# Segment sums of a graph layer: each 128-node tile gathered from three edge blocks by half products into one PSUM bank, instead of one window product per block

## The chip, the cores and the metric

The kernel runs on one core of a Trainium2 chip. The metric is the device time of one execution in microseconds, lower is better. Three runs of the kernel before took 2466.66, 2468.91 and 2469.73 us, so the median is 2468.91 us.

## What is computed

One layer of a graph network over 6250 nodes with 256 channels and 100,000 edges, sorted by their target node, followed by a mixture of experts whose gate is a second graph attention over 131,072 other edges. The part that the change touches is the segment sum in the first half:

```python
msg = relu(x[src] + edge_attr @ We + be)            # one row of 256 per edge
aggr = segment_sum(msg, dst, num_segments=6250)     # rows added up by target node
z = x + aggr
h = relu(relu(z @ W1 + b1) @ W2 + b2) + x           # then a layer norm
```

A linear attention and a wide MLP (the "mixer") run on the same nodes. Their sum is normalised and goes to the second half: a table of 20 numbers per node, gathered once per edge of the second graph, and four experts per node.

## The kernel before

**Stages.** The trace has three parts. Up to about 104 us the nodes are normalised and written to memory, as rows to be gathered (`xb_d`) and as the starting values of the sums (`z0_d`). From there to about 1277 us comes the *edge stage*, which this document is about. It does the edge messages, the sums, the attention, the mixer MLP, the node MLP (`graph_mlp`) and a bitonic sort of the second graph's edge keys, all interleaved. From 1278 us on the second half gathers 784 times from the table `tab_d`, which the edge stage completes as its last act.

**Blocks.** Edges are cut into tiles of 128 and blocks of eight tiles (`EG = 8`); there are 99 blocks (`NQ`). The edge list is shifted by half a block so that block `q` always falls into a fixed *window* of 128 nodes that starts at node 64·(q−1). There are 49 tiles of 128 nodes (`NT`). An odd block `q` covers exactly tile `q // 2`; an even block covers the second half of tile `q // 2 − 1` and the first half of tile `q // 2`. So a tile `k` takes rows from blocks 2k, 2k+1 and 2k+2.

**One block, step by step.** GpSimd (POOL) gathers the source rows, 128 at a time, by indirect DMA (L408, `gather_four`, four to a buffer `xg`, four buffers). TensorE multiplies edge attributes by `We` (L1241) into one of two PSUM buffers `msg`. VectorE adds the gathered rows (L1227, `m`), which frees the `xg` and the `msg` buffer. ScalarE applies the relu (L1229). TensorE then adds up the rows of each tile by slot, with the one-hot matrix `S` (L1259): eight products with 32 columns each fill the four 32-partition quarters of one bank. ScalarE copies that bank to `left` (L1263). `W` is a one-hot matrix of 128 by 128 which places the 128 slots in the window (L1215; for even blocks with the two halves of its columns exchanged, `iotah`). The *window product* `W.T @ left` (L1266) yields the 128 rows of the window in a bank `win`, and VectorE adds them to the sum tile `z` (L1188): one add of 128 rows for an odd block, two adds of 64 rows each for an even one. `graph_mlp` of a group of four node tiles (L1060 to L1176) starts when the last block of the group has been added.

**Order of work.** The engines run their instructions in the order in which the program emits them, and this order is written by a planner at build time (`Plan`, L65 to L130). Each thread of work yields steps with an engine, an assumed length, the slots it takes and drops (`bank`, `left`, `W`, `xg` ...), and names it needs and gives. The planner keeps a clock for each engine and always emits the step that can begin earliest; among steps of the same engine that can begin within 0.3 us (TensorE) or 0.15 us (others), the lowest `rank` goes first. `of_edges` makes the rank of edge steps 0 while the share of edge blocks begun is more than 6% behind the share of node work, and 6 otherwise; the mixer MLP has rank 6, `graph_mlp` rank 1, the sort −1 or 9. A change of a length, a rank or a slot count therefore reorders steps far from where it is made. Slots are counted by the planner, and the buffers behind them (`bufs=`) rotate on the chip, where semaphores hold the real waits. Four PSUM banks serve all products but the messages.

Of the kernel before, what the change touches and what calls it, by code (L numbers as in the profile page):

```python
# [8 lines left out]
F32 = mybir.dt.float32  # L9
# [8 lines left out]
P = 128  # L18
D = 256
# [15 lines left out]
GW = 4  # L35
EG = 8
# [10 lines left out]
PE, DVE, ACT, POOL, SP, MEM = range(6)  # L47
# [3 lines left out]
def mm(n, cols):  # L51
    return n * max(0.25, 0.00185 * cols)


def vec(cols, n=1):
    return n * (0.15 + 0.00105 * cols)


def act(cols, n=1):
    return n * (0.2 + 0.00084 * cols)  # L60


class Plan:
# [12 lines left out]
    def spawn(self, thread, at=0.0):  # L76
        step = next(thread, None)
        if step is not None:
            self.threads.append([thread, step, at, -1])
# [18 lines left out]
    def step(self):  # L98

        can = [(b, t) for t in self.threads for b in [self.begin(t)] if b is not None]  # L100
        if not can:
            assert not self.threads, [t[1] for t in self.threads]
            return False
        first, t = min(can, key=lambda c: c[0])
        near = first + (0.3 if t[1]["on"] == PE else 0.15)

        def rank(c):
            r = c[1][1].get("rank", 5)
            return r() if callable(r) else r

        b, t = min((c for c in can if c[1][1]["on"] == t[1]["on"] and c[0] <= near), key=lambda c: (rank(c), c[0]))
        thread, st = t[0], t[1]
        for k in st.get("take", ()):
            self.slots[k].remove(min(self.slots[k]))
        self.table = st.get("table") or self.table
        end = b + st["length"]
        self.free[st["on"]] = end
        t[2], t[3] = end + LAG[st["on"]], st["on"]
        at = len(self.threads)
        t[1] = next(thread, None)  # L120
        for k in st.get("give", ()):
            self.when[k] = t[2]
        for k in st.get("drop", ()):
            self.slots[k].append(t[2])
        for new in self.threads[at:]:
            new[2] = max(new[2], t[2])
        if t[1] is None:
            self.threads.remove(t)
        return True
# [7 lines left out]
def gps_layer_kernel(ctx: ExitStack, tc: tile.TileContext, a: dict, out: bass.AP):  # L137
    nc = tc.nc
    N = a["x"].shape[0]
    NQ = a["eaQ"].shape[0]  # L140
    NE = a["gat_dst"].shape[0]
    NT = (N + P - 1) // P
    NG = (NT + GW - 1) // GW
    NU = NQ * EG
    NUE = a["srcT"].shape[1]
    assert NUE % 2 == 0 and NU - EG < NUE <= NU
    CG = NE // P

    chunks = [(o, CW) for o in range(0, SURE - CW * P, CW * P)]
# [5 lines left out]
    def rows(t):  # L155
        return min(P, N - t * P)

    def group(g):
        t0 = g * GW
        nt = min(GW, NT - t0)  # L160
        return t0, nt, min(GW * P, N - t0 * P)
# [14 lines left out]
    def bank(name):  # L176
        return general[0].tile([P, 512], F32, tag="bank", name=name)
# [116 lines left out]
    WIN = P // 2  # L294
    EA, ZB = 3, 3
# [4 lines left out]
    ew = res.enter_context(tc.tile_pool(name="edge_w", bufs=3))  # L300
# [111 lines left out]
    XG = 4  # L412
    zs, eas, xgs = {}, {}, {}
# [78 lines left out]
    for g in range(NG + 3):  # L492
# [13 lines left out]
        if 0 <= g - 2 < NG:  # L506
            k = g - 2
# [3 lines left out]
            for o in range(KD):  # L511
                ps = bank("xmid")
                for c in range(KD):
                    nc.tensor.matmul(ps[:, :cols], wx[:, c, o * P:(o + 1) * P], yT[:, c, :cols],
                                     start=c == 0, stop=c == KD - 1)
                nc.scalar.activation(xm[:, o, :cols], ps[:, :cols], AF.Identity, bias=bx[:, o:o + 1])
        if 0 <= g - 3 < NG:
            k, cols = g - 3, group(g - 3)[2]
# [7 lines left out]
        if 0 <= g - 2 < NG:  # L526
            k, cols = g - 2, group(g - 2)[2]
# [34 lines left out]
        if 4 <= g < 8:  # L562
            s = slice(32 * (g - 4), 32 * (g - 4) + 32)
# [8 lines left out]
    for o in range(KD):  # L572
        nc.tensor.matmul(pr[:, o * P:(o + 1) * P], kmax[:, o:o + 1].to_broadcast([P, P]), ident,
                         start=True, stop=True)
# [89 lines left out]
    def sort():  # L664
# [72 lines left out]
        for w in sorted({w for _, w in chunks}, reverse=True):  # L737
            first = [o for o, w_ in chunks if w_ == w]
            o0 = first[0]
            for o in first:  # L740
                if o == first[-1] or o + w * P not in first:
# [11 lines left out]
    xms.update({(0, g): x_mids[g] for g in first_order[:2]})  # L753
    R4, NXH = 7, 4
    plan = Plan(dict(bank=4, msg=2, xm=0, x=NXH, x_=1, hm=NXH, hm_=1, r4=R4, hT=1, qT=2, xn=1, mv=6,
                     xg=XG - 0, ea=EA, S=2, W=2, m=2, left=2, z=ZB))
    plan.when.update({("xm", 0, g): 0.0 for g in first_order[:2]})
    spawn = plan.spawn
    NODES = NT * 14.9
# [418 lines left out]

    kinds, mss = {}, {}

    def add_sums(pw, k, p0, p1):

        if not 0 <= k < NT:
            return
        p1 = min(p1, rows(k))
        if p0 < p1:
            z = zs[k // GW]
            nc.vector.tensor_add(z[p0:p1, k % GW, :], z[p0:p1, k % GW, :], pw[p0:p1, :D])  # L1188

    def sum_loads():  # L1190
        for g in range(NG):
            yield step(SP, 0.4, take=["z"], give=[("z", g)], rank=3)
            load_sums(g)
# [13 lines left out]
    def block_kinds():  # L1207

        for q in range(NQ):
            yield step(DVE, vec(256) + vec(64), take=["S", "W"], give=[("kinds", q)], rank=2)  # L1210
            S = ew.tile([P, EG, SLOT], F32, tag="S", name="S", bufs=2)
            nc.vector.tensor_tensor(S, iotaf[:, :SLOT].unsqueeze(1).to_broadcast([P, EG, SLOT]),
                                    slot[:, q * EG:(q + 1) * EG].unsqueeze(2).to_broadcast([P, EG, SLOT]), OP.is_equal)
            W = ew.tile([P, P], F32, tag="W", name="W", bufs=2)
            nc.vector.tensor_scalar(W, iotaf if q % 2 else iotah, spot[:, q:q + 1], None, op0=OP.is_equal)  # L1215
            kinds[q] = S, W

    def halves(q):
        return [(s, [i for i in range(4 * s, 4 * s + 4) if tile_ok(q * EG + i)]) for s in range(2)
                if tile_ok(q * EG + 4 * s)]  # L1220
# [22 lines left out]

    def sums():

        for q in range(NQ):
            hs = halves(q)
            tiles = [i for _, got in hs for i in got]
            assert len(tiles) % 2 == 0
            p0, p1 = tiles[0] // 2 * SLOT, (tiles[-1] // 2 + 1) * SLOT  # L1250
            yield step(PE, 1.1, need=[("m", q, s) for s, _ in hs] + [("kinds", q)], take=["bank"],
                       rank=of_edges, drop=["m"] * len(hs) + ["S"])
            S, W = kinds.pop(q)
            ps = bank("ps")
            ms = {s: mss.pop((q, s)) for s, _ in hs}
            for b in range(2):
                for i in tiles[b::2]:
                    j = i // 2
                    nc.tensor.matmul(ps[j * SLOT:(j + 1) * SLOT, :D], S[:, i, :], ms[i // 4][:, i % 4, :],  # L1259
                                     start=b == 0, stop=b == 1)  # L1260
            yield step(ACT, act(256), take=["left"], drop=["bank"], rank=0)
            left = ew.tile([P, D], F32, tag="left", name="left", bufs=2)
            nc.scalar.activation(left[p0:p1], ps[p0:p1, :D], AF.Copy)  # L1263
            yield step(PE, mm(1, 256), take=["bank"], drop=["left", "W"], rank=of_edges)
            pw = bank("win")
            nc.tensor.matmul(pw[:, :D], W[p0:p1, :], left[p0:p1, :], start=True, stop=True)  # L1266
            yield step(DVE, vec(256, 1 if q % 2 else 2), drop=["bank"], rank=1, give=[("sums", q)],
                       need=[("z", min(k // GW, NG - 1)) for k in ([q // 2] if q % 2 else [max(q // 2 - 1, 0), q // 2])])
            if q % 2:
                add_sums(pw, q // 2, 0, P)  # L1270
            else:
                add_sums(pw, q // 2 - 1, P // 2, P)
                add_sums(pw, q // 2, 0, P // 2)

    for thread in (block_loads(), gathers(), messages(), sums(), block_kinds(), node_loads(), sum_loads(),
                   mid_loads(), weights(), head_weights(), mid_weights(), mixer_mlp(), sort(), clears()):
        spawn(thread)
# [499 lines left out]
    spawn = plan.spawn  # L1777
# [88 lines left out]
def program(arrays):  # L1866
    import concourse.bacc as bacc

    nc = bacc.Bacc("TRN2", target_bir_lowering=False, num_devices=1)
    aps = {k: nc.dram_tensor(f"in_{k}", v.shape, mybir.dt.from_np(v.dtype), kind="ExternalInput").ap()  # L1870
           for k, v in arrays.items()}
    out = nc.dram_tensor("out", arrays["x"].shape, F32, kind="ExternalOutput").ap()
    with tile.TileContext(nc) as tc:
        gps_layer_kernel(tc, aps, out)
    return nc
# [9 lines left out]
```

## Time and profile before

| | |
|---|---|
| median of three runs | 2468.91 us |
| the profiled execution, its own time | 2467.7 us |
| its span, first to last instruction | 2465.9 us |
| mean granted TensorE clock | 0.912 |
| edge gathers (POOL, L408) | 782, mean 1017 ns, busy 795.1 us |
| window products (PE, L1266) | 99, two records each, busy 66.3 us in 128-row form |
| sum adds (DVE, L1188) | 147: 97 of 64 rows, 48 of 128, one each of 106 and 42; median 414 ns |
| copies of a block's slots (ACT, L1263) | 99, median 383 ns |

How to read it: "busy" is the time an engine spends in instructions. PE is TensorE's matmul, PEld its weight load, DVE VectorE, ACT ScalarE, POOL GpSimd and SP the engine that issues most plain DMAs. A float32 matmul of this kernel leaves two records, so "x8" is four products. An idle time is followed by an arrow and the instruction whose end released the engine; "issue" means that nothing in the profile held it. The chain of waits is followed back from the last instruction, at each step to what released it.

### The profile page before, as it was taken

The numbers are of one execution on the slowest core, as the hardware profiler recorded it, in microseconds if no ns is written. First come the engines' busy times: TensorE is split into PE (matmuls) and PEld (weight loads), VectorE is DVE, ScalarE is ACT, GpSimd is POOL, SyncE is SP. The second block draws the span as 40 slices with busy tenths as digits, with TensorE's granted clock in tenths as the row PEclk, the third lists the DMA queues.
The fourth block names the chain that finished last, engine by engine and source line by source line (L and its number), as shares of the span: only waits on it lengthen the run. The fifth ranks groups of instructions, "written<-read, shape, count | busy, mean of one in ns | idle before, by whom it ended". The sixth has DMA issues, their size and how long they took to land.

```text
span 2465.9 us, 30623 instructions
## 1 busy us (share of the span) xinstructions
PE 1997.3 (81%) x10156; PEld 1297.9 (53%) x10156; DVE 1590.8 (65%) x4328; ACT 898.9 (36%) x1429; POOL 1703.3 (69%) x1701
## 2 busy tenths in 40 slices
PE   6897889998899898999969999978578898986000
PEld 3484555565565565566546776644245565655000
DVE  7588886674687786888736771119757456426566
ACT  5544645555555455665521002112222131212001
POOL 5417777777677777777327777777777777777771
PEclk9998999999999998999989999989789999998555
DMA  8865457767655545554341111212335445224522
GB/s 261 283 198 177 141 156 226 225 192 241 205 148 152 159 132 166 155 149 122 93 133 25 13 46 52 62 45 78 85 95 181 113 137 167 67 57 113 176 50 72
DMA packets 243957, 329.65 MB, mean 134 GB/s; under 512 B 49504, under 2 KB 187010, under 8 KB 242374
## 3 DMA queue, kind: packets, MB, share of 16 engines
q1 hardware_dynamic: 176678, 209.82, 26.1%
q0 software_dynamic: 65776, 116.46, 19.1%
q8 instruction: 84, 1.38, 0.2%
q10 hardware_dynamic: 1328, 1.26, 0.2%
q14 instruction: 91, 0.75, 0.1%
HBM read 227.34 MB, written 100.04 MB: 133 GB/s over the span
## 4 chain that ended last, share of the span: by engine, by line
POOL 35%; PE 25%; issue 14%; DVE 10%; DMA 9%; ACT 2%; SPq 0%; DVEq 0%; POOLq 0%; ACTq 0%
POOL G L1329 22%; POOL xg L408 9%; DMA xg<-xb_d,srcI 6%; PE hist L1491 5%; PE ffn L1040 3%; DVE m L1227 3%; PE msg L1241 3%; PE ffn L1056 3%; PE e L1629 2%; POOL st_d L1563 2%; POOL gm L1653 2%; PE e L1611 2%; PE g L1093 1%; PE ps L1259 1%; PE g L1082 1%
## 5 line engine op out<-in xcount | busy, mean ns | idle before, releaser
L408 POOL DMA_INDIRECT xg<-xb_d,srcI x782 | 795.1, 1017 | 314.3 <-issue 208.1
L1329 POOL DMA_INDIRECT G<-tab_d,srcs x784 | 768.5, 980 | 317.5 <-issue 238.6
L1589 ACT ACTIVATE hT<-e,w_eb 128x512 f32<-128x512 f32 (+1 forms) x208 | 136.3, 661 | 732.8 <-PE e L1629 712.0
L1629 PE MATMUL e<-lT,ew 128*128 128x512 f32 (+1 forms) x832 | 365.9, 587 | 17.6 <-DMA lT<-xlT_d 10.4
L1611 PE MATMUL e<-ew,hT 128*128 128x256 f32 (+1 forms) x1568 | 364.4, 389 | 4.0 <-DVE yo L1593 1.6
L1611 PEld LDWEIGHTS e<-ew,hT 128*128 128x128 f32 (+1 forms) x1568 | 302.5, 195 | 68.8 <-issue 21.1
L1227 DVE TENSOR_TENSOR m<-msg,xg 128x1024 f32<-128x1024 f32 x196 | 234.1, 1217 | 128.3 <-DMA xg<-xb_d,srcI 78.0
L1229 ACT ACTIVATE m<-m 128x1024 f32<-128x1024 f32 x196 | 205.7, 1053 | 187.9 <-DVE m L1227 184.4
L1241 PE MATMUL msg<-we,ea 64*128 64x256 f32 x1564 | 225.6, 415 | 48.7 <-DVE m L1227 43.6
L1629 PEld LDWEIGHTS e<-lT,ew 128*128 128x128 f32 x832 | 153.7, 195 | 178.8 <-issue 152.6
L1593 DVE TENSOR_TENSOR yo<-e,b 128x256 f32<-128x256 f32 (+1 forms) x196 | 79.0, 419 | 233.2 <-PE e L1611 233.1
L1241 PEld LDWEIGHTS msg<-we,ea 64*128 64x128 f32 x1564 | 143.5, 194 | 130.3 <-DVE m L1227 88.7
L1341 PE MATMUL cT<-ident,T 128*4 128x128 f32 (+1 forms) x42 | 13.4, 319 | 223.1 <-DVE T L1411 70.4
L1040 PE MATMUL ffn<-yT,w_mW1T 128*128 128x512 f32 (+1 forms) x416 | 191.3, 587 | 1.0 <-ACT hT L1030 0.5
L1056 PE MATMUL ffn<-w_mW2T,hT 128*128 128x256 f32 (+1 forms) x784 | 187.5, 387 | 0.0
L1056 PEld LDWEIGHTS ffn<-w_mW2T,hT 128*128 128x128 f32 (+1 forms) x784 | 146.0, 191 | 36.9 <-issue 15.2
L1501 DVE TENSOR_TENSOR oh<-iotar,hl 128x1024 bf16<-128x1024 bf16 (+1 forms) x256 | 123.1, 555 | 43.4 <-PE hist L1491 43.4
L1491 PE MATMUL hist<-oh 128*64 128x128 bf16 x1024 | 125.7, 418 | 9.5 <-DMA b<-in_eb 9.5
L1341 PEld LDWEIGHTS cT<-ident,T 128*4 128x4 f32 (+1 forms) x42 | 3.6, 86 | 232.1 <-issue 121.0
L1259 PE MATMUL ps<-m,S 128*32 128x256 f32 x1564 | 110.0, 397 | 15.4 <-ACT yT L1018 7.7
L1491 PEld LDWEIGHTS <-oh 128*64 128x64 bf16 x1024 | 101.6, 198 | 37.0 <-issue 12.6
L1040 PEld LDWEIGHTS ffn<-yT,w_mW1T 128*128 128x128 f32 x416 | 74.7, 195 | 73.6 <-issue 67.2
(382 smaller groups left out, 2909.9 us busy)
## 6 DMA issues: line engine op xcount, KB each, us to landing
ea<-in_eaQ SPq DMA_DIRECT2D x99, 256.0 KB
y_d<-yo SPq DMA_DIRECT2D x48, 512.0 KB
y<-y_d SPq DMA_DIRECT2D x48, 512.0 KB
sum_d<-zf SPq DMA_DIRECT2D x32, 512.0 KB
G<-tab_d,srcs POOLq DMA_INDIRECT x784
xg<-xb_d,srcI POOLq DMA_INDIRECT x782
xm<-xmT_d SPq DMA_DIRECT2D x23, 512.0 KB
sum_d<-G SPq DMA_DIRECT2D x11, 1024.0 KB
```

The source lines that it names most:

```text
L408: nc.gpsimd.indirect_dma_start(out=xg, out_offset=None, in_=xb_d[:, :], in_offset=bass.IndirectOffsetOnAxis(ap=srcI[:, u:u + 1], axis=0))
L1040: nc.tensor.matmul(ps[:, :cols], mw1[:, k, c * P:(c + 1) * P], yTs[g][:, k, :cols], start=k == 0, stop=k == KD - 1)
L1056: nc.tensor.matmul(ps[:r, :D], hT[0][:, c, i * P:i * P + r], mw2[:, c, :], start=c == 0, stop=c == MC - 1)
L1227: nc.vector.tensor_add(m[:, :n, :], ps[:, :n, :], xgs.pop(q * EG + 4 * s)[:, :n, :])
L1229: nc.scalar.activation(m[:, :n, :], m[:, :n, :], AF.Relu)
L1241: nc.tensor.matmul(ps[:, i % 4, :], lh, rh, start=True, stop=True)
L1259: nc.tensor.matmul(ps[j * SLOT:(j + 1) * SLOT, :D], S[:, i, :], ms[i // 4][:, i % 4, :], start=b == 0, stop=b == 1)
L1329: nc.gpsimd.indirect_dma_start(out=rows_of[o][:, c, :], out_offset=None, in_=tab_d[:, :], in_offset=bass.IndirectOffsetOnAxis(ap=srcs[:, o ...
L1491: nc.tensor.matmul(hist[0][b * KHI:(b + 1) * KHI, :P], hi[:, :, b * HG // 2 + i], lo[:, :, b * HG // 2 + i], start=c0 + i == 0, stop=c0 + ...
L1589: nc.scalar.activation(hT[:, c, :cols], ps[:, :cols], AF.Gelu, bias=b1[:, e * XC + c:e * XC + c + 1])
L1611: nc.tensor.matmul(ps[:r, :D], hT[:, c, i * P:i * P + r], w2s[e][:, c, :], start=c == 0, stop=c == XC - 1)
L1629: nc.tensor.matmul(ps[:, :cols], w1s[e][:, k, c * P:(c + 1) * P], lTs[g][:, k, :cols], start=k == 0, stop=k == KD - 1)
```

## The change

The window product and its adds are taken out of the loop over blocks. The loop now only keeps each block's `W` and `left`. Behind every even block from the second on, a new thread `by_node(k)` makes tile `k` whole: four products with 64 columns each (two column halves `h`, two terms `b`), each taking one half of a block's `W`, accumulate in one bank: rows 0 to 63 from blocks 2k and 2k+1, rows 64 to 127 from blocks 2k+1 and 2k+2. One add of all the tile's rows puts it in `z`. The TensorE step of `by_node` has rank 1 and an assumed length of 1.1 us; before, the window product had the rank of the edges and a length of 0.474 us per block. The buffers `left` grow from two to four and `W` from two to five. In the first and the last block, whose slots fill only 64 and 32 rows, `left` is first set to zero on VectorE, since the half products read all 128 rows. The name `("sums", q)` is given for even blocks only, which are the only ones that are asked for. No DMA is added, taken away or written differently.

```diff
-    plan = Plan(dict(bank=4, ..., S=2, W=2, m=2, left=2, z=ZB))
+    plan = Plan(dict(bank=4, ..., S=2, W=5, m=2, left=4, z=ZB))
...
-    def add_sums(pw, k, p0, p1):
-
-        if not 0 <= k < NT:
-            return
-        p1 = min(p1, rows(k))
-        if p0 < p1:
-            z = zs[k // GW]
-            nc.vector.tensor_add(z[p0:p1, k % GW, :], z[p0:p1, k % GW, :], pw[p0:p1, :D])
...
-            W = ew.tile([P, P], F32, tag="W", name="W", bufs=2)
+            W = ew.tile([P, P], F32, tag="W", name="W", bufs=5)
...
     def sums():
+        lefts = {}
+
+        def by_node(k):
+            yield step(PE, 1.1, take=["bank"], drop=["left", "W"] * 2, rank=1)
+            pw = bank("win")
+            for b in range(2):
+                for h in range(2):
+                    W, left = lefts[2 * k + b + h]
+                    s = slice(h * WIN, (h + 1) * WIN)
+                    nc.tensor.matmul(pw[s, :D], W[:, s], left, start=b == 0, stop=b == 1)
+            yield step(DVE, vec(256), drop=["bank"], rank=1, need=[("z", k // GW)], give=[("sums", 2 * k + 2)])
+            r = rows(k)
+            z = zs[k // GW][:r, k % GW, :]
+            nc.vector.tensor_add(z, z, pw[:r, :D])
...
-            yield step(ACT, act(256), take=["left"], drop=["bank"], rank=0)
-            left = ew.tile([P, D], F32, tag="left", name="left", bufs=2)
+            yield step(ACT, act(256), take=["left"], drop=["bank"], rank=0, give=[("sums", 0)] if q == 0 else [])
+            left = ew.tile([P, D], F32, tag="left", name="left", bufs=4)
+            if p1 - p0 < P:
+                nc.vector.memset(left, 0.0)
             nc.scalar.activation(left[p0:p1], ps[p0:p1, :D], AF.Copy)
-            yield step(PE, mm(1, 256), take=["bank"], drop=["left", "W"], rank=of_edges)
-            pw = bank("win")
-            nc.tensor.matmul(pw[:, :D], W[p0:p1, :], left[p0:p1, :], start=True, stop=True)
-            yield step(DVE, vec(256, 1 if q % 2 else 2), drop=["bank"], rank=1, give=[("sums", q)],
-                       need=[("z", min(k // GW, NG - 1)) for k in ([q // 2] if q % 2 else [max(q // 2 - 1, 0), q // 2])])
-            if q % 2:
-                add_sums(pw, q // 2, 0, P)
-            else:
-                add_sums(pw, q // 2 - 1, P // 2, P)
-                add_sums(pw, q // 2, 0, P // 2)
+            lefts[q] = W, left
+            if q and q % 2 == 0:
+                spawn(by_node(q // 2 - 1))
```

More of the change, by code (lines that the diff above doesn't have):

```diff
@@ L145, in gps_layer_kernel @@
     NUE = a["srcT"].shape[1]
-    assert NUE % 2 == 0 and NU - EG < NUE <= NU
+    assert NUE % 2 == 0 and NU - EG < NUE <= NU and NQ == 2 * NT + 1
     CG = NE // P
@@ L755, in gps_layer_kernel @@
     plan = Plan(dict(bank=4, msg=2, xm=0, x=NXH, x_=1, hm=NXH, hm_=1, r4=R4, hT=1, qT=2, xn=1, mv=6,
-                     xg=XG - 0, ea=EA, S=2, W=2, m=2, left=2, z=ZB))
+                     xg=XG - 0, ea=EA, S=2, W=5, m=2, left=4, z=ZB))
     plan.when.update({("xm", 0, g): 0.0 for g in first_order[:2]})
```

## The prediction

> **What bounds the kernel now.** I read the busy time by stage first, since the change touches only the edge stage (104 to 1277 us).
>
> ```profile
> core 0: us, PE busy (x) PEld busy (x) DVE busy (x) ACT busy (x) POOL busy (x), PEclk, DMA share, GB/s
> 155.00:300.00 145.00, 123.51 (x812) 84.26 (x811) 125.58 (x249) 77.76 (x124) 93.82 (x90) 0.94 0.55 163
> 450.00:600.00 150.00, 137.66 (x848) 85.14 (x844) 90.59 (x178) 83.75 (x127) 111.44 (x115) 0.97 0.75 227
> 750.00:900.00 150.00, 135.35 (x814) 86.59 (x815) 118.66 (x216) 80.17 (x121) 115.56 (x114) 0.94 0.50 146
> 900.00:1050.00 150.00, 137.02 (x822) 85.84 (x821) 121.33 (x230) 86.08 (x129) 115.84 (x113) 0.95 0.51 153
> 1211.00:1270.00 59.00, 57.28 (x248) 39.22 (x246) 27.45 (x81) 24.12 (x47) 0.00 (x0) 1.00 0.15 45
> ```
>
> POOL looks 77% busy, but 114 gathers in 150 us are one every 1.32 us, and the timeline of POOL shows 0.30 us of its own issue ahead of each. So 114 gathers of 1.014 us and 114 issues of 0.30 us make 149.8 of 150 us: from 750 to 1050 us POOL never waits. PE is 91% busy, DVE 80%. Who held POOL after 190 us:
>
> ```profile
> POOL xg L408 <- issue: 200.2, 657, 0.3
> POOL xg L408 <- DVE m L1227: 26.2, 21, 6.4
> POOL xg L408 <- DMA xg<-xb_d,srcI: 8.8, 29, 0.3
> ```
>
> Waits of 0.3 us are the issue time under another name. Real stops are only those above 0.5 us: 4.87 us ending at 373, 4.64 at 449, 4.12 at 535, 6.44 at 622 and 1.20 at 1091, together 21.3 us. Two earlier stops of 20.9 and 23.6 us end at 156 and 185 us; there the plan does the attention's first part ahead of the messages, and the sums have hardly begun (first add at 180 us). So the gather stream sets the pace until its last gather at 1200 us, and no help for DVE can bring the edges forward by more than 21 us. Behind it the last row of the table is a tail of TensorE work, 57.28 busy of 59 us, mostly mixer MLP left over by the plan's order. The second half starts when `tab_d` is complete and is again a stream of gathers (158 in each 200 us), unchanged, so what the edge stage gains or loses goes one to one into the time.
>
> **DVE's part: 98 adds fewer.**
>
> ```profile
> L1188 DVE TENSOR_TENSOR z<-z,win x147: 387/414/426, 180.2 to 1220.1; 64x256 f32<-64x256 f32 x97, 128x256 f32<-128x256 f32 x48, 106x256 f32<-106x256 f32 x1, 42x256 f32<-42x256 f32 x1
>   PE win L1266: 36.9, 25
> ```
>
> An add of 64 rows costs as much as one of 128 (418 and 412 ns in the groups by shape). Now 49 remain: 98 × 0.414 = 40.6 us of DVE are gone, 4% of the stage. The question is what of it lay on the path. I summed the pieces of the chain of waits from 104 to 1283 us, in short windows so that none is left out: POOL L408 212.6 us, the gathers' DMA 149.2, issue 136.4, PE L1040 75.5, DVE L1227 70.5; for what the change touches, PE L1266 17.4, DVE L1188 8.9, ACT L1263 0.7. Even the 8.9 is too much, as this piece of the chain shows:
>
> ```profile
> 1148.78 0.34 DVE z L1188
> 1149.13 0.06 issue
> 1149.18 4.18 DMA xg<-xb_d,srcI
> ```
>
> The chain goes from a gather to an add that has nothing to give it: a 0.3 us issue gap put down to whatever ended then. The list of POOL's waits has 8 such waits on L1188 (2.4 us in all); 8 × 0.41 = 3.3 us come off, leaving 5.6. Two thirds of the adds go (98 of 147): **−3.7 us**.
>
> Would fewer adds also make the gathers themselves shorter? They are stretched: after 190 us their time above 0.95 us adds up to 52.5 us. Rows of POOL and DVE side by side:
>
> ```profile
> 254.41 2.10 POOL L408 DMA_INDIRECT xg<-xb_d,srcI  x1 [0.30 <-issue]
> 254.41 0.68 DVE L677 TENSOR_TENSOR key<-key 128x512 f32<-128x512 f32 x1
> 199.51 0.95 POOL L408 DMA_INDIRECT xg<-xb_d,srcI  x1 [0.30 <-DMA xg<-xb_d,srcI]
> 198.31 2.34 DVE L1227 TENSOR_TENSOR m<-msg,xg 128x1024 f32<-128x1024 f32 x2
> ```
>
> Beside the sort's min and max, with both inputs in SBUF, a gather takes 2.10 us; beside the `m` add, one input in PSUM, 0.95. The Trainium skill (SBUF — State Buffer, "Who interferes with whom") says the same of instructions with at most one SBUF input, that they do not contend with GpSimd; it also infers that a two-input `tensor_tensor` spares descriptor generation, which these rows speak against. The removed add reads `z` from SBUF and `win` from PSUM, so it is of the sparing kind. If all of DVE's work stretched gathers alike, 52.5 × 40.6 / 805 (DVE busy, 155 to 1211 us) = 2.6 us would be gained; by row and rule it is 0. I take 0.
>
> **PE's part: 99 whole products become 196 half products.** From the start of a window product to the start of the next PE instruction, where PE did not idle, is 0.55 us (87 cases in the timeline): 99 × 0.55 = 54.5 us. No row shows a float32 product with 64 columns. From above: if the halves don't overlap, four at 0.43 us (a 256-column product at full clock: 32 of L1056 in 13.83 us) and 0.14 us around them are 1.86 us a tile. From below: two column halves run side by side, as the slot sums L1259 do with four quarters: eight products, 8 × 0.43 / 4 = 0.86 us of streaming, take 1.00 us from start to start (91 cases). A tile is then 4 × 0.43 / 2 = 0.86, and 0.14 for entering and leaving the narrower form: 1.00. L1259 has the same column tiling, alternating targets and bank, so I take 1.00: 49 × 1.00 = 49.0, PE −5.5 us. Of PE L1266 17.4 of 54.5 us (32%) lay on the chain: **−1.8 us**.
>
> A rule speaks against this: TensorEngine Tiling (Array Packing), "Key Properties", says that changing the tiling mode drains TensorE, and L1266 stood in the same 128x128 mode as most of its neighbours. It gives no price; TensorE: Matmul & The Clock Gate, "Single matmul latency", puts an isolated product at (398 + N) cycles against N, an estimate of 0.17 us a drain. Two drains a tile make 0.86 + 0.33 = 1.19 us, 58.3 us in all, +3.8 on PE, +1.2 on the chain: the total would be −2.5, no measurable change. The row has two such switches within its 0.14, so I keep the row.
>
> **The rest, at nothing.** Two memsets of 256 columns: between 0.06 us (128x8) and 0.46 us (128x480), under 1 us in all, off the gathers' path; if the last one came late it would hold one ACT copy of the last node tile, behind which 50 us of PE tail still run. 49 PSUM banks fewer are taken of four; PE's idle before L1259 (the next taker) is 15.4 us in all, so at most that, part of the same stalls; I take 0. The longer life of `left` and `W` is covered by four and five buffers: tile k holds three blocks, one more `left` and two `W` are free. The bank waits for ACT's newest copy: PE and PEld stood 8.5 us in 17 of 99 waits on it. By rank 1 the products now come right behind the copy. Bounds: none left (−8.5 × 0.32 = −2.7 on the chain), or 0.5 us at each of 49 tiles (24.5, +16 × 0.32 = +5). Behind them in PE's queue stand messages, behind those the `m` adds that free `xg`. I take 0, as there are half as many such waits. No DMA, SP or POOL instruction is moved by itself.
>
> **Sum.** −3.7 − 1.8 = −5.5 on the profiled execution's own 2467.7 us (span 2465.9 and 1.8 around it): 2462.2. The median of the runs is 1.2 us above that execution, so 2463.4.
>
> **Rivals.** Of this kernel no change under about 0.2% (4.9 us) can be told from none.
>
> *The gather stream hides it.* For: 149.8 of 150 us in mid-stage, and DVE itself waits for gathered rows (78.0 us in 34 waits of L1227). The 40 us turn into longer waits of that kind. 2468, from −4.9 to +4.9 of the median.
>
> *Slower: new stops of POOL.* The plan is dealt anew with shorter DVE and other ranks. The four stops of 4.1 to 6.4 us each come where two `m` adds stand in DVE's queue behind adds that wait for PE (L1104 behind L1093, 32.7 us in 7 waits). The new add waits for four products that wait for ACT, and stands at rank 1; L1188 already waited 36.9 us in 25 waits. Where it stands ahead of an `m`, POOL stops once its four buffers are full. Each stop costs about 5 us, so from two new ones on the sign turns; three give −5.5 + 15: 2478. Against: half as many adds, and most of mid-stage had no stop in spite of 147.
>
> *The halves don't overlap.* 49 × 1.86 = 91.1, +36.6 on PE, × 0.32 = +11.7, less 3.7: 2477. Against: L1259.
>
> *The old stops vanish too.* −5.5 − 20: 2443. Against: L1188 hardly takes part in them (one add of 0.42 us ahead of the first stop).
>
> **How the numbers follow.** Likeliest, 0.39: 2463.4, about 2453 to 2464. Hidden 0.28; new stops 0.22; no overlap 0.06; old stops gone 0.05. Faster 0.39 + 0.05 = 0.44, same 0.28, slower 0.28. The range runs from just inside the vanished stops, 2445, to four new stops, −5.5 + 20: 2484.
>
> **What would show it.** L1188's successor with 49 adds near 0.414 us and DVE some 40 us less busy; the half products at 1.00 us a tile from start to start; gathers unchanged near 1.02 us mean; POOL's stops after 190 us near 21 us, last gather near 1195 to 1200; the PE tail behind it near 60 us. I am wrong if stops come or go by more than 5 us, if the tail's length changes with the new order, or if a tile costs 1.5 us or more on PE.

## The result, and the profile after

The changed kernel takes 2489.01 us (median of four runs, 2485.28 to 2490.55) against 2468.25 us for the kernel before, run beside it (four runs): ratio 1.0089, 95% interval 1.0069 to 1.0109. It is 21 us slower, where 2463.4 was predicted and 2484 was the top of the range.

The profiled execution took 2490.55 us, its span is 2488.7. The busy time by stage, in the columns shown before, with two rows more: 950 to 1180 us, and the tail from the last edge gather to the second half. The changed kernel first:

```profile
core 0: us, PE busy (x) PEld busy (x) DVE busy (x) ACT busy (x) POOL busy (x), PEclk, DMA share, GB/s
155.00:300.00 145.00, 124.92 (x818) 87.58 (x818) 120.53 (x235) 74.37 (x122) 91.80 (x88) 0.92 0.52 159
450.00:600.00 150.00, 140.60 (x900) 84.29 (x901) 85.52 (x162) 84.85 (x130) 114.39 (x117) 0.97 0.77 230
750.00:900.00 150.00, 132.91 (x853) 83.38 (x853) 117.98 (x208) 80.86 (x121) 115.91 (x112) 0.96 0.49 145
900.00:1050.00 150.00, 132.07 (x864) 80.04 (x865) 116.00 (x219) 83.19 (x127) 115.03 (x115) 0.98 0.53 158
950.00:1180.00 230.00, 207.25 (x1326) 125.02 (x1325) 178.56 (x324) 133.59 (x201) 176.06 (x178) 0.98 0.49 146
1191.00:1301.00 110.00, 92.73 (x415) 61.30 (x413) 47.68 (x134) 46.39 (x85) 1.19 (x3) 0.96 0.16 47
```

The two added rows in the kernel before:

```profile
950.00:1180.00 230.00, 221.88 (x1366) 143.96 (x1366) 194.86 (x370) 138.95 (x211) 177.33 (x170) 1.00 0.48 143
1200.00:1278.00 78.00, 71.22 (x322) 46.22 (x320) 40.74 (x111) 34.20 (x67) 1.10 (x1) 0.97 0.18 50
```

The POOL column is nearly as before: gathers still set the pace. The PE column is what differs. From 950 to 1180 us TensorE is busy for 14.6 us less, and the tail behind the gathers holds 21.5 us more of its work. The POOL timeline shows the joint itself, first after, then before:

```profile
1191.38 0.95 POOL L408 DMA_INDIRECT xg<-xb_d,srcI  x1 [0.30 <-issue]
1300.83 0.94 POOL L1331 DMA_INDIRECT G<-tab_d,srcs  x1 [108.51 <-DVE iotar L1474]
```

```profile
1200.27 1.10 POOL L408 DMA_INDIRECT xg<-xb_d,srcI  x1 [0.30 <-issue]
1278.48 0.95 POOL L1329 DMA_INDIRECT G<-tab_d,srcs  x1 [77.12 <-DVE iotar L1472]
```

The last edge gather comes 8.9 us *earlier*, and the second half starts 22.4 us *later*. The tail has grown from 78.2 to 109.4 us. The second half itself takes 1187.9 us against 1187.4, so the joint holds the whole loss.

What the change meant to do, it did. The groups of VectorE, after, with the sums and with the message adds:

```profile
L1251 DVE TENSOR_TENSOR z<-z,win 128x256 f32<-128x256 f32 (+1 forms) x49 | 20.2, 413 | 21.5 <-DMA z<-z_d 11.5 <-PE win L1247 9.9
L1218 DVE TENSOR_TENSOR m<-msg,xg 128x1024 f32<-128x1024 f32 x196 | 236.8, 1219 | 177.7 <-DMA xg<-xb_d,srcI 125.8 <-PE ps L1266 42.5 <-PE win L1247 3.3
```

The 49 adds take 413 ns each, and VectorE is busy 1554.3 us instead of 1590.8. The relieved engine waits longer for gathered rows (125.8 us for 78.0). A tile of half products takes 1.01 us from its start to the start of the next TensorE instruction (median of the 39 cases without idle time).

One note on the runs below: e1 to e4 ran beside a kernel before at 2469.55 us (the *first setting*), while from e5 on the kernel before took 3651 to 3687 us with a mean granted clock of 0.77 to 0.78 (the *second setting*), so every ratio is to the kernel before that ran beside it on the same chip. The chip numbers on record are 15, 3, 10, 0 and 2 in the second setting and 0 for e1 to e4, so the record does not tell whether the chip or its condition makes the difference. In the second setting TensorE idles for up to 20 us at a time with no releaser in the trace (last section), and POOL is stopped for over 320 us in all after 190 us (19.8 before, in the first setting), so gathers do not set the pace there.

### The profile page after: what moved, and what is told of

It reads as the page before. It is cut to its first block, busy times and chain, and to the rows that moved or that the text cites. A ratio compares the mean times of both kernels' runs of the same rounds, so it can differ in the third digit from the quotient of the medians.

```text
span 2488.7 us, 30841 instructions
## 1 busy us (share of the span) xinstructions
PE 2005.8 (81%) x10350; PEld 1286.3 (52%) x10350; DVE 1554.3 (62%) x4232; ACT 905.2 (36%) x1434; POOL 1696.1 (68%) x1701
## 5 line engine op out<-in xcount | busy, mean ns | idle before, releaser
L408 POOL DMA_INDIRECT xg<-xb_d,srcI x782 | 788.0, 1008 | 312.0 <-issue 210.6
L1218 DVE TENSOR_TENSOR m<-msg,xg 128x1024 f32<-128x1024 f32 x196 | 236.8, 1219 | 177.7 <-DMA xg<-xb_d,srcI 125.8
L1056 PE MATMUL ffn<-w_mW2T,hT 128*128 128x256 f32 (+1 forms) x784 | 188.2, 387 | 0.7 <-ACT hT L1030 0.7
L1056 PEld LDWEIGHTS ffn<-w_mW2T,hT 128*128 128x128 f32 (+1 forms) x784 | 143.1, 189 | 42.4 <-issue 23.1
```

The lines of the kernel that those rows point to most:

```text
L408: nc.gpsimd.indirect_dma_start(out=xg, out_offset=None, in_=xb_d[:, :], in_offset=bass.IndirectOffsetOnAxis(ap=srcI[:, u:u + 1], axis=0))
L1056: nc.tensor.matmul(ps[:r, :D], hT[0][:, c, i * P:i * P + r], mw2[:, c, :], start=c == 0, stop=c == MC - 1)
L1218: nc.vector.tensor_add(m[:, :n, :], ps[:, :n, :], xgs.pop(q * EG + 4 * s)[:, :n, :])
```

## The experiments

**Which theory.** A: the re-dealt order costs the time. The half products' step has rank 1, where the window product had the rank of the edges (0 or 6). Edges run ahead of node work, and node work is left for the time behind the last gather. B, the rival: the new work itself costs the time (four products that wait for the newest copy, an add that waits for all four).

A can be put in a number without a run. In the emitted order of TensorE's instructions I counted the columns of all node products (mixer, attention, node MLP, with their transposes) behind the last message product, at 0.43 us for 256 columns, as in the 13.83 us for 32 of L1056. That is 59 us before and 85 us after. This number is called the *backlog* below. The two orders agree in this count up to about message tile 640 of 782, and part from there (162 against 171 us left at 640, 103 against 120 at 720).

### e1: the change's work in the order of before

```diff
...
+            whole = q % 2 == 0 and k >= 0
+            if whole:
+                pw = bank("win")
+                for b in range(2):
+                    for h in range(2):
+                        W_, left_ = lefts[2 * k + b + h]
+                        s = slice(h * WIN, (h + 1) * WIN)
+                        nc.tensor.matmul(pw[s, :D], W_[:, s], left_, start=b == 0, stop=b == 1)
...
```

The steps, lengths, ranks and slots of before; every even block emits the 4 half products and the one add, an odd block emits nothing. The cut parts are the change's buffers, its two memsets and the one add.

> The changed work (196 half products, 49 adds, two memsets) emitted at the planner's steps of the kernel before, so that every other instruction stands in the old order: 59 us of node products stand behind the last message product on TensorE, as before (85 in the changed kernel). Theory A (the new order costs the time, the new work itself saves some): 2459 to 2466 us, gathers end near 1191 to 1197 us, tail behind them near 78 us. Rival B (the half products, the memsets or the longer chain from three copies to one add cost the time): 2480 to 2492 us, as the changed kernel.

Measured: 2457.85 us (2445.87 to 2461.71), ratio 0.9951 (0.9934 to 0.9968). The POOL timeline at the joint:

```profile
1185.11 0.95 POOL L408 DMA_INDIRECT xg<-xb_d,srcI  x1 [0.30 <-issue]
1259.66 0.94 POOL L1337 DMA_INDIRECT G<-tab_d,srcs  x1 [73.61 <-DVE iotar L1480]
```

The tail is 74.6 us, as with the order before (78.2), and the last gather is 15 us earlier. B falls: the same work, in the old order, makes the kernel 12 us *faster*. (The execution with the trace, 2445.87 us, is the fastest of six, 12 us under their median; so the rows of e1 show more gain than its runs have in the middle.)

### e2: the removed adds put back

```diff
             nc.vector.tensor_add(z, z, pw[:r, :D])
+            n = min(r, WIN)
+            for _ in range(2):
+                nc.vector.tensor_add(pw[:n, D:], z[:n], pw[:n, :D])
```

The 98 added adds write into the unused half of the bank, and nothing reads them.

> The changed kernel in its own order, with two more adds of 64 rows by 256 per node tile on VectorE (98 in all), whose results go to an unused half of the PSUM bank and are not read; so VectorE has its old load in the new order. Theory A: the 40 us of adds are worth 0 to 9 us also here, so 2489 to 2498 us. Rival (VectorE's relief is what set the edges ahead and so made the tail longer on the chip): the time falls towards 2468.

Measured: 2501.44 us (2495.42 to 2503.9), ratio 1.0131 (1.0116 to 1.0147). That is 0.42% over the changed kernel by the two ratios, some 10 us, a little more than either theory said; the execution with the trace (2495.42 us, the fastest of four) is only 4.9 us over that of the changed kernel. The tail stays (110.4 us). So the adds are worth about as much in the new order as in the old, and the tail does not depend on them.

### e3: another assumed gather length

```diff
-            yield step(POOL, 5.0, take=["xg"], give=[("xg", u)])
+            yield step(POOL, 5.27, take=["xg"], give=[("xg", u)])
```

No work changes. Only the planner's clock of POOL runs slower, nearer to four gathers and four issues as measured (4 × (1.017 + 0.30) = 5.27 us). The backlog falls from 85 to 52 us.

> The changed kernel with one number of the planner changed: four gathers are assumed to take 5.27 us (4 x 1.317 as the trace of before has them) instead of 5.0. The work is the same; 52 us of node products stand behind the last message product instead of 85. Theory A: the tail gets shorter by about 20 to 33 us and the gathers end no more than 10 us later: 2456 to 2475 us. Rival B: 2485 to 2492.

Measured: 2440.91 us (2435.73 to 2448.03), ratio 0.989 (0.9873 to 0.9907), below the expected interval and faster than both kernels. The tail is 65.2 us, the last gather at 1181.3, and the stops of POOL after 190 us fall from 16.2 to 8.9 us. The order alone is worth 48 us against the changed kernel.

### e4: the kernel before, with rank 1 alone

```diff
-            yield step(PE, mm(1, 256), take=["bank"], drop=["left", "W"], rank=of_edges)
+            yield step(PE, mm(1, 256), take=["bank"], drop=["left", "W"], rank=1)
```

> The kernel before with one word changed: the window product's step has rank 1 as in the change, not the rank of the edges. The work is the kernel before's; 70 us of node products stand behind the last message product instead of 59. Theory A: slower by about 6 to 14 us, 2474 to 2482. Rival B: no change, 2466 to 2471.

Measured: 2492.48 us (2491.49 to 2493.35), ratio 1.0092 (1.0079 to 1.0105). Nothing of the change's work is in this kernel, and the loss is as large as that of the change. By stage (950 to 1180 us, and the tail):

```profile
950.00:1180.00 230.00, 212.23 (x1313) 134.93 (x1312) 187.82 (x349) 136.09 (x209) 174.29 (x171) 0.98 0.51 151
1206.00:1301.00 95.00, 81.35 (x349) 51.90 (x348) 43.16 (x122) 45.45 (x83) 0.51 (x1) 0.91 0.16 49
```

TensorE shows the pattern of the changed kernel: 9.7 us less busy than before from 950 to 1180, and 10.1 us more in the tail, with a tail of 95.8 us. It was slower than expected, because the tail's idle time grew too (13.7 us against 6.8), which the backlog does not count, and because the last gather came 5.3 us later, where the changed kernel has it 8.9 us earlier.

The runs of the first setting side by side, each from its execution with the trace. Stops are POOL's waits above 0.5 us after 190 us, less 0.3 us of issue each; gathers are L408's busy time:

| | backlog | stops | gathers | last gather | tail | second half starts | ratio |
|---|---|---|---|---|---|---|---|
| before | 59 | 19.8 | 795.1 | 1200.3 | 78.2 | 1278.5 | 1 |
| after | 85 | 16.2 | 788.0 | 1191.4 | 109.4 | 1300.8 | 1.0089 |
| e1 | 59 | 19.9 | 780.6 | 1185.1 | 74.6 | 1259.7 | 0.9951 |
| e2 | 85 | 15.9 | 795.1 | 1193.7 | 110.4 | 1304.1 | 1.0131 |
| e3 | 52 | 8.9 | 787.6 | 1181.3 | 65.2 | 1246.5 | 0.9890 |
| e4 | 70 | 22.2 | 795.0 | 1205.6 | 95.8 | 1301.3 | 1.0092 |

The last gather follows stops plus gathers: e1 has 14.5 us less of gathers and ends 15.2 us earlier; e3 has 18.4 us less of both and ends 19.0 earlier. The tail follows the backlog, with 13 to 26 us on top.

### The second setting: e5 to e18

Here the question was how far the backlog decides by itself. Times that were expected for the first setting could not be tried. (The expectation of e10 gives 395 us of stops for e6 and 308 to 323 for e5 and e7; counted as in the table above they are 476, and 355 and 387.)

**e5, e9, e15: 5.27 in the kernel before** (backlog 30; the edit of e3).

> The kernel before with one number changed: the planner takes 5.27 us instead of 5.0 for a gather of four; no work is changed. In the emitted order 30 us of TensorE node work stand behind the last message product, against 59 before. Theory A (the node work left behind the last gather is what decides): the last gather stays near 1195 to 1203, the tail to the second half falls from 78 to 45 to 55 us, the time is 2430 to 2452. Rival B (the gain with 5.27 came from something that only the new sums have, shorter gathers or half products): 2462 to 2475, no change.

> The kernel before with 5.27 us for a gather of four in the planner, again, on another chip: the first run stood on a chip on which the kernel before takes 3679 us and POOL is stopped 300 us in all by late TensorE and DVE. Node work behind the last message product: 30 us, against 59 before. Theory A (the node work left behind the last gather decides): tail 45 to 55 us, time 2430 to 2452. Rival B (the gain with 5.27 needs the new sums): 2462 to 2475.

> The kernel before with 5.27 us for a gather of four in the planner. Where the kernel before takes 3650 to 3680 us: 0.986 to 0.990 of it, as in two runs. Where it takes 2469 us: theory A (30 us of node work behind the last message product instead of 59) tail 45 to 55 us, 2430 to 2452; rival B (the gain with 5.27 needs the new sums) 2462 to 2475.

Measured: 3633.75, 3628.09 and 3638.79 us; ratios 0.9896 (0.9851 to 0.9941), 0.9863 (0.9836 to 0.9891) and 0.987 (0.9848 to 0.9893). The tails are 55.2, 56.6 and 55.0 us. Rival B of these runs, that the gain needs the new sums, falls at least in this setting.

**e6, e10, e12, e16: the changed kernel with the rank of the edges** (backlog 8).

```diff
-            yield step(PE, 1.1, take=["bank"], drop=["left", "W"] * 2, rank=1)
+            yield step(PE, 1.1, take=["bank"], drop=["left", "W"] * 2, rank=of_edges)
```

> The changed kernel with one word changed: the half products' step has the rank of the edges instead of 1; no work is changed. 8 us of TensorE node work stand behind the last message product. Theory A: with the rank of the edges the loss goes, and the tail is the shortest of all, 25 to 40 us. How far the last gather moves back is the question: if TensorE takes the node work in its idle time, it stays below 1215 and the time is 2405 to 2440; rival B (edges now come too late, POOL is stopped by TensorE, and the last gather moves back by what the tail loses): last gather 1230 to 1255, stops above 30 us, time 2445 to 2475.

> The changed kernel with the half products at the rank of the edges, on a chip where gathers set the pace. 8 us of node work stand behind the last message product. Theory A: tail 25 to 40 us, last gather below 1215, time 2405 to 2440. Rival B (edges come too late, POOL is stopped, the last gather moves back by what the tail loses): last gather 1230 to 1255, stops after 190 us above 30 us, time 2445 to 2475. On the slow chip POOL's stops were 395 us here, against 308 to 323 of e5 and e7, and the time was 1.2% above before; that speaks for B.

> The changed kernel with the half products at the rank of the edges, once more, for a chip where gathers set the pace (the kernel before at 2469 us). 8 us of node work stand behind the last message product. Theory A: tail 25 to 40 us, last gather below 1215, time 2405 to 2440. Rival B (edges come too late, POOL is stopped, the last gather moves back by what the tail loses): last gather 1230 to 1255, stops after 190 us above 30 us, time 2445 to 2475. Where the kernel before takes 3680 us, the runs say 1.010 to 1.012 of it.

> The changed kernel with the half products at the rank of the edges. Where the kernel before takes 3650 to 3680 us: 1.010 to 1.015 of it, as in three runs, the last gather 80 to 110 us later than in e13. Where it takes 2469 us: theory A tail 25 to 40 us, last gather below 1215, 2405 to 2440; rival B (edges too late, POOL stopped) last gather 1230 to 1255, 2445 to 2475.

Measured: 3721.28, 3719.4, 3706.98 and 3719.65 us; ratios 1.0117 (1.0091 to 1.0144), 1.0096 (1.0068 to 1.0125), 1.0149 (1.0099 to 1.0198) and 1.0096 (1.0074 to 1.0117). The tail is the shortest of all, 38 to 41 us, and still the kernel is the slowest: the last gather comes at 1606 to 1621 us. POOL's waits in e16, then in the changed kernel in this setting (e13); columns are total, times and longest:

```profile
POOL xg L408 <- DVE m L1218: 493.5, 70, 23.5
```

```profile
POOL xg L408 <- DVE m L1218: 393.1, 69, 23.3
```

The edges now come too late, and POOL loses 100 us. Rival B holds here. So the one-word repair is no repair in this setting, and a short tail is not worth having at any price.

**e7, e11: rank 1 for the first nine tenths of the tiles, then the rank of the edges** (backlog 59).

```diff
-            yield step(PE, 1.1, take=["bank"], drop=["left", "W"] * 2, rank=1)
+            yield step(PE, 1.1, take=["bank"], drop=["left", "W"] * 2, rank=1 if k < 0.9 * NT else of_edges)
```

> The changed kernel with the half products at rank 1 for the first nine tenths of the tiles and at the rank of the edges for the last tenth; no work is changed. Its order is that of the changed kernel up to about message 760 of 782; 59 us of node work stand behind the last message product, as in the kernel before, against 85. Theory A in its simple form (what stands behind the last message decides): 26 us less tail, 2458 to 2470. Rival A2 (what decides is whether TensorE finds node work in its idle time during the last fifth of the edge stage; moving it across the last messages only moves the last gather back): last gather 1200 to 1215, tail 80 to 95, time 2478 to 2490.

> The changed kernel with rank 1 for the first nine tenths of the tiles and the rank of the edges for the last tenth, on a chip where gathers set the pace. 59 us of node work stand behind the last message product, as before, but up to message 760 of 782 the order is that of the changed kernel. Theory A in its simple form: last gather 1190 to 1200, tail 78 to 84, 2458 to 2470. Rival A2 (moving node work across the last messages only moves the last gather back, since TensorE is the bound there; what decides is the node work missing over the last fifth): last gather 1200 to 1215, tail 80 to 95, time 2478 to 2490.

Measured: 3691.73 and 3694.67 us; ratios 1.0036 (1.0021 to 1.0052) and 1.0034 (1.002 to 1.0048). The tails are 88.7 us in both, the last gathers at 1535 and 1541. Against the changed kernel (e13 below) the tail is 34 us shorter, and the last gather comes 23 and 29 us later: moving node work across the last messages mostly moved the last gather back, as rival A2 said.

**e8: 5.4 in the changed kernel** (backlog 42).

```diff
-            yield step(POOL, 5.0, take=["xg"], give=[("xg", u)])
+            yield step(POOL, 5.4, take=["xg"], give=[("xg", u)])
```

> The changed kernel with the planner's length for a gather of four at 5.4 us instead of 5.0; no work is changed. 42 us of node work behind the last message product, against 52 with 5.27 and 85 with 5.0. Theory A: tail 53 to 62 us, last gather 1180 to 1195, time 2425 to 2442. Rival: with gathers taken as longer than they are the edges come late and POOL stops more (over 20 us after 190), 2442 to 2465.

Measured: 3631.46 us, ratio 0.9878 (0.9853 to 0.9904). The tail is 73.5 us, the last gather at 1490.6, the earliest of all in this setting. It is again faster than before, and on a par with e5.

**e13, e14: the changed kernel and e1 once more** (backlogs 85 and 59).

> The changed kernel as it is, beside the others on their chip. Where the kernel before takes 3650 to 3680 us (there TensorE and DVE stop POOL for over 300 us and the gathers no longer set the pace) theory A, the tail: about 115 us from the last gather to the second half, where 30 us of node work behind give 56, 59 give 89; ratio 1.002 to 1.010. Rival C (the re-dealt order costs only where gathers set the pace): the work saved shows, ratio 0.990 to 0.998. Where the kernel before takes 2469 us: 2485 to 2491, as measured.

> The change's work in the order of before, beside the others on their chip. Where the kernel before takes 3650 to 3680 us: theory A 0.990 to 0.997 of it (98 adds and 5 us of TensorE less, with the tail of before); rival C (order does not matter there) the same ratio as e13. Where the kernel before takes 2469 us: 2450 to 2460, as measured.

Measured: 3696.98 and 3691.14 us; ratios 1.0025 (1.0008 to 1.0042) and 1.0023 (1.0005 to 1.0041). The tails are 122.6 and 83.9 us, the last gathers at 1512.4 and 1546.9 us. What e13 has more in the tail, e14 has ahead of the last gather, nearly one for one. So the old order is worth nothing where gathers do not set the pace, and neither is the work saved. Theory A as I put it for this setting (at least 0.5% between the two) was wrong, and so was C's expectation of a gain; C's other half, the same ratio for both, held.

**e17, e18: what shortened the gathers.** The first table has the gathers 7 to 15 us shorter with 49 adds than with 147. e17 is the kernel before with the change's buffers alone; e18 is e2 with copies that do not read SBUF:

```diff
-            W = ew.tile([P, P], F32, tag="W", name="W", bufs=2)
+            W = ew.tile([P, P], F32, tag="W", name="W", bufs=5)
...
-            left = ew.tile([P, D], F32, tag="left", name="left", bufs=2)
+            left = ew.tile([P, D], F32, tag="left", name="left", bufs=4)
```

```diff
-                nc.vector.tensor_add(pw[:n, D:], z[:n], pw[:n, :D])
+                nc.vector.tensor_copy(pw[:n, D:], pw[:n, :D])
```

> The kernel before, order and work unchanged, with the change's buffers only: five W instead of two, four left instead of two. In every run so far the 782 gathers sum to 790.1 to 796.6 us with 147 adds (or 49 and 98 added ones) and to 773.6 to 789.4 us with 49. If the adds make the difference, 789 to 797 here; if the place or number of the buffers does, 773 to 785. Time within 0.4% of before by the first, up to 0.5% less by the second where gathers set the pace.

> The changed kernel with 98 extra VectorE copies of 64 rows from PSUM to PSUM, at the places at which e2 had adds that also read z from SBUF; nothing reads the copies. e2 had gathers of 795.2 us in all, the changed kernel 789.4 (and 777.3 on the slower chips). If any instruction of VectorE at those places lengthens the gathers: 786 to 796. If it is the read of SBUF that e2's adds have: 774 to 783 (or 786 to 790 where the kernel before takes 2469 us, and then 2487 to 2496).

Measured: 3687.98 us, ratio 0.9997 (0.9983 to 1.0012), and 3710.38 us, ratio 1.0059 (1.0046 to 1.0072). The groups of the gathers in e17, e18 and the changed kernel e13, in this setting (busy, then mean ns):

```profile
L408 POOL DMA_INDIRECT xg<-xb_d,srcI x782 | 786.2, 1005 | 655.5 <-DVE m L1227 420.5 <-issue 212.6 <-SPq L434 6.8
```

```profile
L408 POOL DMA_INDIRECT xg<-xb_d,srcI x782 | 785.2, 1004 | 648.1 <-DVE m L1218 397.5 <-issue 215.7 <-DVE nm L263 8.2
```

```profile
L408 POOL DMA_INDIRECT xg<-xb_d,srcI x782 | 776.0, 992 | 645.1 <-DVE m L1218 393.1 <-issue 215.5 <-DVE rs L262 8.0
```

(The sums in the expectations are made from the rounded rows of the timeline and stand 1 to 2 us above these; e17's is 787.5, e18's 786.4.) With 98 copies that read PSUM alone the gathers are 9.2 us longer than in e13, so the lengthening does not need a read of SBUF. With the buffers alone they are still 10.2 us longer than in e13, and 2 to 5 us under the kernel before with 5.27 (788.6 to 790.8 in e5, e9 and e15); e17 fell between its two expected intervals, so a small part for the buffers stays possible. One pair proves little, as kernels with the same 49 adds differ by up to 7.4 us in the first setting (e1 and after). But the two kinds stand apart in every trace: in the second setting 785.2 to 790.8 us with the old number of instructions (e5, e9, e15, e17, e18) and 772.3 to 780.8 with 49 adds alone (the nine others); in the first 795.0 to 795.1 and 780.6 to 788.0. The number of instructions is the greater part.

The timelines also show where the difference lies: in the few long gathers. Those above 1.5 us number 12 to 20 in each trace with the old number of instructions and 4 to 9 in each with 49 adds alone (before 20, after 9, e1 8, e2 17). Where these were looked up, most of the additional ones run beside the sort's min and max (`key`), whose inputs both lie in SBUF.

## Why the prediction was wrong, point by point

**The step that failed: the change's order, put at nothing.** Under "the rest, at nothing" the prediction looked at rank 1 only for the wait on ACT's copy, and the sum kept before's tail of about 60 us of TensorE work. The last paragraph named the tail's length as what would prove it wrong, but no term had a price for it. e4 shows that the rank by itself brings the loss (1.0092 against 1.0089), and e1 that the work without the rank brings a gain (0.9951). The mechanism: at rank 1 the step beats the mixer (rank 6) wherever both can begin, while the rank of the edges is itself 6 as long as edges are not behind. The plan then lets edges go first. TensorE's waits from 950 to 1180 us show what that does, in before, after and e4 (us in total, times, longest):

```profile
PE msg L1241 <- DVE m L1227: 0.8, 2, 0.5
PE msg L1232 <- DVE m L1218: 14.6, 12, 3.2
PE msg L1241 <- DVE m L1227: 7.0, 4, 2.4
```

Message products stand in TensorE's queue ahead of node work and wait for a PSUM buffer, which an `m` add frees; that add waits for gathered rows (22.2 us in 15 waits in this stretch, 2.9 in 4 before, 14.4 in 10 in e4). With the order of before, in e1, the message products wait 1.3 us for `m` adds. (In e3 they wait 8.5 us, but its order has less node work left by then: 150 us behind message tile 640, against 162 before and 171 after.) So TensorE is 14.6 us less busy there, and does the node work behind the last gather, where no gather runs beside it. The chain of waits at the end of the changed kernel's tail shows what this work is (pieces under 0.4 us left out; before ends in the like lines):

```profile
1269.37 1.90 PE ffn L1040 x4
1271.27 0.57 PE hg L1158 x16
1271.85 1.91 PE ffn L1040 x4
1273.87 3.44 PE ffn L1040 x8
1277.31 13.83 PE ffn L1056 x64
1291.16 0.43 DVE hm L1046
1291.61 0.70 DVE z L1127
```

But for the heads (`hg`) and the last add (`z`), it is mixer work that needs no edge. Of the 25 us by which the backlog is larger than before, 17 are such `ffn` products; the rest are attention products, transposes and heads. Of the 31.2 us by which the tail is longer, 21.5 are TensorE's work, and about 10 are idle time of TensorE. One part of the idle time: the last add waits 11.5 us for its `z` (the L1251 group above), and TensorE stands 4.39 us for that add before 1233.52 us. The load stands in SP's queue behind the store of the sorted keys and a store of `x_d` at 1221 us and the loads of the sorted keys, and goes at 1227.34; before, the like load went at 1187.73. No run took that queue apart, so its share of the loss is argued only; e4, with the same loss, waits for such loads 1.7 us in all.

**Mis-sized: the gathers' own stretching, taken as 0.** Row and rule agreed that an add with one SBUF input spares the gathers, and a single `m` add in the trace did. But e1 has the gathers 14.5 us shorter in all, nearly all of the 15.2 us by which its last gather is earlier (in its fastest execution, see there), and e2 brings back 7.1 of the changed kernel's 7.1. The average that the prediction set aside (2.6 us, by VectorE's busy time) was too low as well. In a fit of each gather's excess to what VectorE did beside its first 0.95 us, the sums have no weight beyond the error of the fit (at most 0.05 us per us), so the gathers that became shorter are not simply those that lay beside a removed add; the sort's `key` instructions, which the change does not touch, have 0.15 to 0.24 us for each us beside a gather. How an instruction lengthens gathers that it does not lie beside stays open.

**Mis-sized the other way: VectorE's −3.7 and TensorE's −1.8 on the chain.** With the order kept, e1's stops are 19.9 us against 19.8, so neither brought the last gather forward through fewer stops; the chain of waits had handed POOL's issue gaps and DMA waits to other engines. Behind the last gather e1's tail is 3.6 us shorter, which may hold some of TensorE's saving. The total of −5.5 for the work was −12 by e1, mostly for another reason than the one given.

**Right, or nearly:** the half products at 1.00 us a tile (1.01), so TensorE's saving (56.5 to 51.1 us from start to start, without idle time); the drain of the array at a change of tiling, priced at 0.33 us a tile against the row, did not show: 1.01 us leave 0.15 over the 0.86 us of streaming; adds at 0.414 us (0.413); VectorE 36.5 us less busy (40 predicted); stops near 21 (with the issue time left out, 19.8 before and 16.2 after); last gather near 1195 to 1200 (1191).

**The slower rival** named the re-dealt plan, rightly, but priced it as new stops of POOL. Stops became fewer. The halves do overlap, so that rival is out, and the gather stream did not hide the gain: e1 is faster.

**What stays open:** whether the rank of the edges would be too late also where gathers set the pace; how 98 short instructions lengthen gathers; and what slows the kernel in the second setting.

## What to carry to other kernels

Where a planner writes the order, a rank or a length is part of the change's cost: emit both orders and count what each engine still has to do behind the last piece of the pacing stream, before pricing any instruction. In this kernel what was added to the tail behind the last gather counted whole, as the second half took the same 1188 us. The count alone does not decide: the order with the least work left behind (8 us, e6) was the slowest, because it stopped the gathers. A plan's assumed lengths are worth measuring: 5.27 us for four gathers instead of 5.0, as this trace had it, was worth more (−48 us from the changed kernel) than all the work that the change saved.

## What the runs showed of the hardware that was not expected

- With 98 short VectorE instructions more, 0.42 us each, the 782 indirect gathers took 7 us (e2 against after) and 9 us (e18 against e13) longer in all, with or without a read of SBUF; the difference lies in gathers above 1.5 us, mostly beside instructions of VectorE with both inputs in SBUF.
- Four products of 128x64 by 256 in float32, in two column halves, took 1.01 us a tile, mostly between neighbours in the 128x128 form, about the 1.00 us of eight products with 32 columns.
- In the second setting the same kernel before took up to 49% longer, with idle times of TensorE of up to 20 us that have no cause in the trace, for instance ahead of weight loads in e17 (the first two lines; columns as for waits). The last two are the same waits of the kernel before in the first setting:

```profile
PEld e L1629 <- issue: 381.7, 618, 19.5
PEld e L1611 <- issue: 316.4, 143, 20.2
PEld e L1629 <- issue: 152.6, 614, 0.5
PEld e L1611 <- issue: 21.1, 85, 0.4
```
